# Quantisation of the feed-forward weights: started in batch 0, paced by five steps in later odd batches, its loads on SyncE's queue

## The chip, the cores and the metric

The kernel runs on one core of a Trainium2 chip. The metric is the device time of one execution in microseconds, as the median of several runs. A core has five engines that run their own instruction streams in order and wait for each other by semaphores: TensorE (PE in the profile; its weight loads are PEld), VectorE (DVE), ScalarE (ACT), GpSimd (POOL) and SyncE (SP), which here only issues transfers. GpSimd issues transfers too; those travel on another DMA queue (q0) than SyncE's (q1).

## The reference, cut to what matters

One block of a Perceiver: cross attention of 64 latents to 512 context rows in each of 16 batches, then self attention over the latents, then a feed-forward layer with FP4 weights and activations. The feed-forward layer quantises its three weight matrices in blocks of 16:

```python
def fp4_quant_dequant(x):
    xb = x.reshape(shape[:-1] + (shape[-1] // BLOCK, BLOCK))
    scale = jnp.max(jnp.abs(xb), axis=-1, keepdims=True) / 6.0
    scale = jnp.maximum(scale, jnp.float32(1e-12))
    idx = jnp.searchsorted(_MID, jnp.abs(xb / scale))
    return (_GRID[idx] * jnp.sign(xb) * scale).reshape(shape)

gate, y = fp4_linear(x, w_gate), fp4_linear(x, w_up)      # 512 -> 1408
return fp4_linear(jax.nn.silu(gate) * y, w_down)          # 1408 -> 512
```

The weights do not depend on the activations, so this quantisation can be done at any time before the feed-forward layer. Every large matrix product is computed in three fp32r terms of high and low halves (high x high, high x low, low x high).

## The kernel before, in words

The kernel has four stages in time: the latents (to 82 us), cross attention batch by batch (82 to 550), self attention and feed-forward. All instructions stand in the order in which the Python code emits them (`in_order`, L87), engine by engine; no planner moves them. An engine that waits holds up all that stands behind it on that engine.

Cross attention (`cross_attention`, L869) goes over `b` in 0 to 15. In each batch TensorE does four products for the keys (`keys(b, m)`, tile `pk`), two passes of scores (`scores(b, a)`, tile `sim`, L979), the weighted sum of the batch before (`finish(b - 1)`, tile `av`) and four products for the values (tile `pv`). Odd batches from 3 on also handle the output of an earlier pair of batches: `out_turn` (a transpose on TensorE, tile `ot`), `out_low`, `out_product` (tile `po`), `out_norm` and `out_add`, the last with three operations on GpSimd (L1163 to L1165); `out_moments` in the next even batch reads their result. The results of `keys`, `out_turn`, `out_product` and `values` share three PSUM buffers (`ps_mm`, L83), the scores share two. VectorE empties the keys (L953) and does the first half of the softmax (L1000), ScalarE empties the values (L966) and does the exponentials.

SyncE loads the context for two batches ahead: `nat` (1 MB, L322) for the statistics and four pieces `raw` (256 KB each, `fetch`, L362) of the transposed context, which ScalarE and VectorE or GpSimd split into high and low halves (L370, L376). It also turns the softmax with transposing transfers (`send`, L1050: two per pass, `far`), stores and reloads the row factors (`flat`, L350; `every`, L355), and loads the mask, the queries and the latents of the next batch (`begin`, L906, L908; `latents_values`, L920). `spread` (L339 to L341) computes the row factors on GpSimd at the end of each batch.

The quantisation (`Quantise`, L247) is cut into 35 pieces: for three column chunks of 512, 512 and 384, four pieces each of the gate and of the up matrix, then eleven of the down matrix. A piece is a generator. `tick()` advances every active piece by one step and, if it is time, starts a new one. A batch has ten places for ticks, called steps 1 to 10 here: after `keys(b, 0)`, after `keys(b, 1)`, after the flat rows, after the second scores, after `values(b, 0)`, two after the loads of the next batch, one after `out_product`, one after the fourth fetch, and one at the end of the batch. A piece's work is, by steps: the load of 128 x 512 fp32 weights into one of three buffers (L287, on GpSimd); nothing; a reduce group on VectorE (L199, L201, L202, L203); a multiplication on GpSimd (L205); a mask on VectorE and an activation on ScalarE (L208, L211); nothing; a pair on VectorE (L213, L214); a multiplication on GpSimd (L216); a transpose on VectorE and a copy on ScalarE (L296, L297); a subtraction on VectorE and the store of 512 KB (L299, L301, on GpSimd). The reduce group's operations are small but L199 must wait for the load.

A new piece starts at every fourth tick. The first tick is the last one of batch 0; batch 1 has eight. The last load is issued in step 8 of batch 14, and the last store in step 7 of batch 15.

Of the kernel before, what the change touches and what calls it, by code (L numbers as in the profile page):

```python
# [46 lines left out]
def f32(t):  # L47

    return t.bitcast(F32)
# [197 lines left out]
class Quantise:  # L247
# [3 lines left out]

    EVERY = 4

    def __init__(self, cm, sc, i):
        self.cm, self.sc = cm, sc
        self.jobs = []
        for c, (at, n) in enumerate(CHUNKS):
            for w, name in (("g", "w_gate"), ("u", "w_up")):  # L260
                self.jobs += [(w, c, k, i[name][k * P : (k + 1) * P, at : at + n]) for k in range(KC)]
        for c, (at, n) in enumerate(CHUNKS):
            self.jobs += [
                ("d", c, k, i["w_down"][at + k * P : at + (k + 1) * P, :]) for k in range(n // P)
            ]
        self.jobs.reverse()
        self.clock, self.active = 0, []

    def home(self, w1, w2):
        self.w1, self.w2 = w1, w2  # L270

    def tick(self, new=True):

        if new and self.jobs and self.clock % self.EVERY == 0:
            self.active.append(self.piece(*self.jobs.pop()))
        self.clock += 1
        self.active = [job for job in self.active if next(job, None)]

    def finish(self, all=False):
# [3 lines left out]
    def piece(self, which, c, k, src):  # L283
        cm, nc = self.cm, self.cm.nc
        name, n = f"{which}_{c}_{k}", src.shape[1]
        w = self.w2.tile([P, D], F32, tag="tri", bufs=3, name=f"qw_{name}")[:, :n]
        nc.gpsimd.dma_start(w, src)  # L287
        yield True
        yield True
        for step in cm.fp4_steps(self.w1, w, n, name, True, True):  # L290
            yield True
            if step == "relu":
                yield True
        hl = self.w1.tile([P, 2, D], F32R, tag="q_hl", name=f"qhl_{name}")[:, :, :n]
        hi, lo = hl[:, 0, :], hl[:, 1, :]
        nc.vector.transpose(f32(lo), w)  # L296
        nc.scalar.copy(hi, f32(lo))  # L297
        yield True
        nc.vector.tensor_tensor(lo, f32(lo), f32(hi), ALU.subtract)  # L299
        dst = self.sc.dn[c] if which == "d" else self.sc.gu[which, c]  # L300
        nc.gpsimd.dma_start(dst[:, :, k, :], f32(hl))  # L301
# [567 lines left out]
def cross_attention(tc, cm, sc, i, cw, cx, w1, w2, att, quant):  # L869

    nc = tc.nc
# [19 lines left out]
    def columns_of(r):  # L891

        first = S * (1 - r)
        return slice(first, first + N + S), slice(S - first, S - first + N)
# [27 lines left out]
    def mask(b):  # L922
        if b < B:
            nc.scalar.activation(
                masks[b % 2][:, S : S + N], state[b]["mu"], AF.Identity, bias=cm.masked, scale=MASKED
            )
# [17 lines left out]
    def keys(b, m):  # L944

        k = ends[b, m // 2][:, m % 2, :]
        hi, lo = cx.done[b]
        cols = slice(m * P, (m + 1) * P)
        ps = cm.mm(f"pk_{b}_{m}")
        cm.product(  # L950
            ps, lambda c: (w_k[0][:, c, cols], w_k[1][:, c, cols], hi[:, c, :], lo[:, c, :]), range(KC)
        )
        nc.vector.tensor_tensor(k[:, S : S + N], ps, cx.row[b], ALU.mult)  # L953
        state[b]["k"].append(k)
# [14 lines left out]
    def scores(b, a):  # L969

        st = state[b]
        st["sim", a] = pss = [cm.two(f"sim_{b}_{a}_{r}") for r in range(2)]
        for h in range(2):
            for r in range(2):
                rows = slice(r * S, (r + 1) * S)
                at = columns_of(r)[0].start + h * half
                for c in range(2):
                    m = 2 * a + c
                    nc.tensor.matmul(  # L979
                        pss[r][c * S : (c + 1) * S, h, :half],  # L980
                        lhsT=queries[b % 2][rows, m, :],
                        rhs=st["k"][m][rows, at : at + half],
                        start=True,
                        stop=True,
                    )

    def softmax(b, a):
        st = state[b]
        both = w1.tile([P, 2 * (N + S)], F32, tag="pr", bufs=2, name=f"pr_{b}_{a}")
        st["whole", a] = both  # L990
        st["pr", a] = both.rearrange("p (r n) -> p r n", r=2)

        def two(t):
            return t.rearrange("p (h n) -> p h n", h=2)

        for r, ps in enumerate(st.pop(("sim", a))):
            mask = masks[b % 2][:, columns_of(r)[0]]
            pr = st["pr", a][:, r, :]
            least = cm.small.tile([P, 1], F32, tag="least", name=f"least_{b}_{a}_{r}")
            nc.vector.tensor_tensor_reduce(  # L1000
                two(pr), ps[:, :, :half], two(mask), -1.0, BIG, ALU.add, ALU.min, least
            )
            t = 2 * a + r
            nc.scalar.activation(  # L1004
                pr, pr, AF.Exp, bias=least, scale=-1.0, accum_out=st["tot"][:, t : t + 1]
            )
# [160 lines left out]
    def out_moments(p):  # L1167
        cm.shift(cm.x[p], f"a_{p}", cm.x_mv[:, p, :])
# [8 lines left out]
    def weight_o(k):  # L1177
        raw = raw_o.pop(k)
        cm.split(w_o[0][:, k, :], w_o[1][:, k, :], raw, nc.gpsimd)
# [18 lines left out]
    cx.load(2)  # L1198
    for b in range(B):

        def tick():
            if b:
                quant.tick()

        done = (b - 3) // 2 if b >= 3 and b % 2 else None
        last = b == B - 1
        keys(b, 0)
        if b:
            cx.load(b + 2)
        if last:  # L1210
            att.load("Wq")
            att.load("Wk")
        cx.high(b + 1, 0)
        if b >= 4 and b % 2 == 0:
            out_moments((b - 4) // 2)
        if b > 1:
            tick()
        if done is not None:
            out_turn(done)
        keys(b, 1)  # L1220
        cx.low(b + 1, 0)
        cx.high(b + 1, 1)
        if b:
            join(b - 1, 0)
        if b > 1:
            tick()
        keys(b, 2)
        if b:
            mask(b)
        if done is not None:  # L1230
            out_low(done)
        cx.fetch(b + 2, 0)
        if b == 0:
            for k in range(KC):
                load_o(k)
        cx.flat(b + 1)
        cx.low(b + 1, 1)
        cx.high(b + 1, 2)
        if b:
            join(b - 1, 1)  # L1240
        tick()
        if last:
            att.split("Wq", 0, 1)
        if b == 0:
            scores(b, 0)
            softmax(b, 0)
        keys(b, 3)
        cx.fetch(b + 2, 1)
        if b:
            scores(b, 0)  # L1250
            softmax(b, 0)
        cx.low(b + 1, 2)
        cx.high(b + 1, 3)
        if b:
            finish(b - 1)
            scores(b, 1)
            softmax(b, 1)
            around(b + 1, 1)
            around(b + 2, 0)
        tick()  # L1260
        values(b, 0)
        if b and not last:
            halves(b, 0)
        cx.every(b + 1)
        cx.low(b + 1, 3)
        cx.stats(b + 2, 0)
        tick()
        if last:
            att.split("Wq", 2, 3)
            att.load("Wv")  # L1270
        if b == 0:
            scores(b, 1)
            softmax(b, 1)
            around(b + 1, 1)
            around(b + 2, 0)
        values(b, 1)
        if b == 0:
            halves(b, 0)
        if not last:
            turn_latents(b)  # L1280
            halves(b, 1)
            send(b, 0)
        begin(b + 1)
        latents_values(b + 1)
        cx.fetch(b + 2, 2)
        cx.stats(b + 2, 1)
        tick()
        if last:
            att.norm(0)
            att.split("Wk", 0, 1)  # L1290
        tick()
        if done is not None:
            out_product(done)
        tick()
        values(b, 2)
        if not last:
            send(b, 1)
        cx.fetch(b + 2, 3)
        cx.stats(b + 2, 2)
        tick()  # L1300
        if done is not None:
            out_norm(done)
            out_add(done)
        if b == 0:
            weight_o(0)
            weight_o(1)
        if b == 5:
            att.sa.work()
        if last:
            att.split("Wk", 2, 3)  # L1310
            att.load("Wo")
            att.turn(0)
        values(b, 3)
        cx.stats(b + 2, 3)
        cx.spread(b + 2)
        if b == 0:
            weight_o(2)
            weight_o(3)
        quant.tick()
# [693 lines left out]
```

## Time and profile before

| | us |
|---|---|
| median of 3 runs | 878.34 (876.41 to 878.44) |
| the profiled execution | 878.15 |
| its span, first to last instruction | 876.4 |
| TensorE busy | 859.5 (98%) |
| VectorE busy | 690.3 (79%) |
| ScalarE busy | 486.4 (56%) |
| GpSimd busy | 345.6 (39%) |
| mean granted TensorE clock | 0.996 |

The profile is of one execution on the chip. Some 2 us lie outside its span. A timeline row gives the start, the length, the engine, the source line, the operation, the tiles written and read, shapes, the number of instructions merged and, in brackets, how long the engine sat idle before and what ended that. A row of a table of stretches gives start:end and length, then the busy time and number of instructions of PE, PEld, DVE, ACT and POOL, the granted clock, the DMA engines' share and GB/s. TensorE's ends are modelled, so back-to-back rows overlap slightly. For SyncE a row is the issue of a transfer; its landing is not in the profile.

### The profile page before, as it was taken

How to read it: one execution, taken by the hardware profiler on the slowest of the kernel's cores; microseconds unless marked ns; L12 is line 12 of the kernel's file. 1: busy time of each engine (PE TensorE's matmuls, PEld its weight loads, DVE VectorE, ACT ScalarE, POOL GpSimd, SP SyncE). 2: the span in 40 equal slices, each digit the busy share in tenths (PEclk: the TensorE clock that was granted, in tenths of full speed). 3: DMA queues.
4: the chain of work that ended last, by engine and by line, in shares of the span. 5: the costliest groups of instructions: out<-in, count | busy, mean ns of one | idle time of the engine just before them, and what ended most of it. 6: DMA issues, size and time to landing. Idle time of an engine off the chain costs nothing.

```text
span 876.4 us, 16721 instructions
## 1 busy us (share of the span) xinstructions
PE 859.5 (98%) x6263; PEld 706.9 (81%) x6263; DVE 690.3 (79%) x1457; ACT 486.4 (56%) x847; POOL 345.6 (39%) x413
## 2 busy tenths in 40 slices
PE   9999999999999999999999999999999999999998
PEld 8988777887887777778877877878888888888886
DVE  7734457988789877887897776698998898888876
ACT  5654675766758757667767576544556232332221
POOL 3334144546465474364654733555543120111100
PEclk9999999999999999999999999999999999999999
DMA  7664767775975777668857564150008330000000
GB/s 243 207 229 170 198 183 202 207 190 182 235 186 154 216 211 202 168 177 224 192 148 211 159 162 182 49 193 2 2 1 336 121 144 24 1 13 13 13 13 24
DMA packets 135607, 126.79 MB, mean 145 GB/s; under 512 B 95512, under 2 KB 98472, under 8 KB 134248
## 3 DMA queue, kind: packets, MB, share of 16 engines
q1 hardware_dynamic: 127912, 99.26, 39.2%
q0 software_dynamic: 7616, 26.48, 9.3%
q8 instruction: 49, 0.80, 0.4%
q14 instruction: 30, 0.25, 0.1%
HBM read 84.26 MB, written 25.72 MB: 125 GB/s over the span
## 4 chain that ended last, share of the span: by engine, by line
PE 84%; DVE 7%; POOL 3%; ACT 2%; DMA 2%; issue 1%; DVEq 0%; POOLq 0%; ACTq 0%
PE pv L126 18%; PE pk L126 14%; PE gu L126 14%; PE dn L126 7%; PE sim L979 4%; PE av L1101 3%; PE Wv L126 3%; PE wo L126 3%; PE lv L126 2%; PE Wq L126 2%; PE Wk L126 2%; PE lq L126 2%; PE lk L126 2%; PE po L126 1%; PE ht L176 1%
## 5 line engine op out<-in xcount | busy, mean ns | idle before, releaser
L126 PE MATMUL pv<-xvh,x 128*128 128x512 f32 x512 | 136.9, 399 | 0.3 <-ACT v L966 0.3
L126 PE MATMUL pk<-x,xkh 128*128 128x512 f32 x512 | 127.2, 390 | 0.0
L126 PEld LDWEIGHTS pv<-xvh,x 128*128 128x128 f32 x512 | 95.2, 190 | 26.8 <-issue 7.3
L126 PEld LDWEIGHTS pk<-x,xkh 128*128 128x128 f32 x512 | 95.5, 188 | 19.8 <-issue 0.4
L1004 ACT ACTIVATE pr<-pr,least 128x576 f32<-128x576 f32 x64 | 49.1, 769 | 60.0 <-DVE least L1000 60.0
L953 DVE TENSOR_TENSOR k<-pk,row 128x512 f32<-128x512 f32 x64 | 42.9, 671 | 39.1 <-PE pk L126 31.6
L126 PE MATMUL pv<-xvl,x 128*128 128x512 f32 x256 | 70.0, 396 | 0.0
L126 PE MATMUL pk<-x,xkl 128*128 128x512 f32 x256 | 68.5, 389 | 0.0
L1060 ACT COPY prT<-far 128x1024 uint16<-128x1024 uint16 x60 | 67.3, 1173 | 1.3 <-DMA far<-half 1.3
L126 PE MATMUL gu<-uT,fx 128*128 128x512 f32 (+1 forms) x288 | 66.8, 377 | 0.0
L966 ACT ACTIVATE v<-pv,rs 128x512 f32<-128x512 f32 x64 | 43.9, 685 | 41.1 <-PE pv L126 40.1
L126 PE MATMUL gu<-gT,fx 128*128 128x512 f32 (+1 forms) x288 | 65.8, 376 | 0.0
L376 POOL TENSOR_TENSOR x<-raw,x 128x512 fp32r<-128x512 f32 x32 | 41.8, 1306 | 55.3 <-ACT x L370 47.4
L1040 ACT COPY half<-pr 128x1024 uint16<-128x1024 uint16 x60 | 59.8, 1048 | 0.0
L126 PEld LDWEIGHTS gu<-gT,fx 128*128 128x128 f32 x288 | 52.2, 188 | 7.6 <-ACT fx L134 0.2
L126 PEld LDWEIGHTS pv<-xvl,x 128*128 128x128 f32 x256 | 49.1, 192 | 11.0
L126 PEld LDWEIGHTS gu<-uT,fx 128*128 128x128 f32 x288 | 51.9, 188 | 7.2
L126 PEld LDWEIGHTS pk<-x,xkl 128*128 128x128 f32 x256 | 48.1, 188 | 10.0
L979 PE MATMUL sim<-k,mask 64*64 64x288 f32 x512 | 43.8, 418 | 9.3 <-DVE least L1000 7.9
L1000 DVE CUSTOM_DVE_ANT_0 pr<-sim,mask 128x576 f32<-128x576 f32 x64 | 45.8, 753 | 5.7 <-PE sim L979 2.8
L211 ACT ACTIVATE qe_h<-qe_h,mmagic 128x512 f32<-128x512 f32 (+1 forms) x24 | 16.5, 688 | 59.1 <-DVE qe_h L208 56.9
L126 PE MATMUL dn<-dT,hh 128*128 128x512 f32 x170 | 42.9, 392 | 0.0
(357 smaller groups left out, 1942.1 us busy)
## 6 DMA issues: line engine op xcount, KB each, us to landing
nat<-in_ctx_dram SPq DMA_DIRECT2D x16, 1024.0 KB
raw<-in_ctxT_dram SPq DMA_DIRECT2D x64, 256.0 KB
d_d<-qhl_d POOLq DMA_DIRECT2D x11, 512.0 KB, 3.8
row<-rs_d SPq DMA_DIRECT2D x16, 256.0 KB
g_d<-qhl_g POOLq DMA_DIRECT2D x8, 512.0 KB, 4.4
u_d<-qhl_u POOLq DMA_DIRECT2D x8, 512.0 KB, 4.6
gT<-g_d SPq DMA_DIRECT2D x4, 1024.0 KB
uT<-u_d SPq DMA_DIRECT2D x4, 1024.0 KB
```

The source lines that it names most:

```text
L126: self.nc.tensor.matmul(ps, lhsT=p[i], rhs=p[j], start=start and n == 0, stop=stop and n == last)
L176: self.nc.tensor.transpose(pt[:, c * P : (c + 1) * P], src[:, c * P : (c + 1) * P], self.ident)
L211: nc.scalar.activation(e, e, AF.Relu, bias=self.mmagic, scale=MAGIC)
L376: by.tensor_tensor(lo, self.raw[:, c, :], f32(hi), ALU.subtract)
L953: nc.vector.tensor_tensor(k[:, S : S + N], ps, cx.row[b], ALU.mult)
L966: nc.scalar.mul(v, ps, cx.rs[b][:, t : t + 1])
L979: nc.tensor.matmul(pss[r][c * S : (c + 1) * S, h, :half], lhsT=queries[b % 2][rows, m, :], rhs=st["k"][m][rows, at : at + half], start=Tru ...
L1000: nc.vector.tensor_tensor_reduce(two(pr), ps[:, :, :half], two(mask), -1.0, BIG, ALU.add, ALU.min, least)
L1004: nc.scalar.activation(pr, pr, AF.Exp, bias=least, scale=-1.0, accum_out=st["tot"][:, t : t + 1])
L1040: nc.scalar.copy(half, src[:, h])
L1060: nc.scalar.copy(dst, src)
L1101: nc.tensor.matmul(st["av"][r][rows, a, :], lhsT=prT[:, j, rows], rhs=st["v"][j][:, at : at + S], start=False, stop=j == NJ - 1, skip_grou ...
```

## The change

Four things change. (1) Ticks count from batch 0 on, eight of them there, and batch 1 has all ten; the first load is issued in step 3 of batch 0. (2) A new piece starts when `every` ticks have passed since the last start: 4, but 5 in batches 7, 9, 11 and 13. (3) A piece's load is issued by SyncE instead of GpSimd, and one more empty step stands between it and the reduce group. (4) In batch 0 the first scores and their softmax stand behind `keys(0, 3)`, as they do in all other batches.

By step, loads are issued in batch 0 in steps 3 and 7; in 1, 3, 5, 8 and 12 in steps 1, 5 and 9; in 2, 4, 6, 10 and 14 in steps 3 and 7; in 7 and 11 in steps 2 and 7; in 9 and 13 in steps 4 and 9. The reduce group follows three steps later, so that of a load in step 7 stands in step 10. In batches 2 to 6 all other work of the pieces stands in the same steps as before. The last load is in step 7 of batch 14, the last store in step 7 of batch 15 as before.

In SyncE's order the load of step 1 stands behind `nat`, that of step 3 behind `flat`, of step 5 behind `every`, of step 7 behind `send(b, 0)`, `begin`, `latents_values` and the third fetch and ahead of `send(b, 1)`, and of step 9 behind the fourth fetch and ahead of the next `nat`.

```diff
 class Quantise:
-    EVERY = 4
-
     def __init__(self, cm, sc, i):
 ...
-        self.clock, self.active = 0, []
+        self.every, self.since, self.active = 4, 3, []
 ...
     def tick(self, new=True):
 
-        if new and self.jobs and self.clock % self.EVERY == 0:
+        self.since += 1
+        if new and self.jobs and self.since >= self.every:
             self.active.append(self.piece(*self.jobs.pop()))
-        self.clock += 1
+            self.since = 0
         self.active = [job for job in self.active if next(job, None)]
 ...
     def piece(self, which, c, k, src):
         cm, nc = self.cm, self.cm.nc
         name, n = f"{which}_{c}_{k}", src.shape[1]
         w = self.w2.tile([P, D], F32, tag="tri", bufs=3, name=f"qw_{name}")[:, :n]
-        nc.gpsimd.dma_start(w, src)
+        nc.sync.dma_start(w, src)
+        yield True
         yield True
         yield True
         for step in cm.fp4_steps(self.w1, w, n, name, True, True):
 ...
     for b in range(B):
 
-        def tick():
-            if b:
-                quant.tick()
-
+        tick = quant.tick
+        quant.every = 4 + (b % 2 if 6 < b < 14 else 0)
 ...
-        if b > 1:
+        if b:
             tick()
         if done is not None:
             out_turn(done)
 ...
-        if b > 1:
+        if b:
             tick()
         keys(b, 2)
 ...
-        if b == 0:
-            scores(b, 0)
-            softmax(b, 0)
         keys(b, 3)
         cx.fetch(b + 2, 1)
-        if b:
-            scores(b, 0)
-            softmax(b, 0)
+        scores(b, 0)
+        softmax(b, 0)
         cx.low(b + 1, 2)
```

## The prediction

> **What bounds the kernel now.** I read the page first. TensorE is busy nearly all the time, so a change can only win what TensorE loses now, or lose more.
>
> ```profile
> span 876.4 us, 16721 instructions
> PE 859.5 (98%) x6263; PEld 706.9 (81%) x6263; DVE 690.3 (79%) x1457; ACT 486.4 (56%) x847; POOL 345.6 (39%) x413
> ```
>
> The waits of PE come next. Each row gives total, times and longest. Only the score matmuls (sim) wait for anything that counts: six times for VectorE's softmax, once for a transfer.
>
> ```profile
> PE sim L979 <- DVE least L1000: 7.9, 6, 1.6
> PE sim L979 <- DMA mask<-q_d: 1.4, 1, 1.4
> ```
>
> Then the stretches, one per batch, cut at each batch's first pk matmul (start:end, length, PE busy and so on; the clock follows POOL). These are batches 1, 2, 4, 5 and 10.
>
> ```profile
> 108.18:134.97 26.79, 26.79 (x211) 21.51 (x210) 13.94 (x32) 19.41 (x31) 11.63 (x13) 1.00 0.69 177
> 134.97:164.02 29.05, 27.48 (x212) 21.68 (x210) 24.11 (x55) 20.16 (x32) 13.58 (x16) 1.00 0.69 186
> 193.99:224.50 30.51, 29.05 (x212) 22.59 (x210) 26.67 (x58) 20.41 (x32) 19.13 (x23) 0.94 0.65 181
> 224.50:254.46 29.96, 29.96 (x228) 24.16 (x226) 23.57 (x53) 20.49 (x34) 13.48 (x16) 1.00 0.79 210
> 371.33:398.78 27.45, 27.45 (x211) 21.68 (x210) 23.57 (x56) 19.56 (x32) 16.47 (x22) 1.00 0.67 179
> ```
>
> An even batch has the matmuls of batch 1, which runs without a gap in 26.79 us. Above that, batches 2 to 14 by twos take 2.26, 3.72, 1.77, 1.60, 0.66, 3.78 and 2.16, together 15.95 us. Odd batches 3 to 13 all take 29.96 or 29.97 without a gap. So the loss sits in even batches, and the timelines say why. PE:
>
> ```profile
> 150.96 1.87 PE L979 MATMUL sim<-k,mask 64*64 64x288 f32 x16 [1.56 <-DVE least L1000]
> 209.87 2.19 PE L979 MATMUL sim<-k,mask 64*64 64x288 f32 x16 [1.46 <-DVE least L1000]
> 230.39 1.98 PE L126 MATMUL pk<-x,xkh 128*128 128x512 f32 x8
> ```
>
> An undisturbed sim pass takes 1.20, so each stall costs its gap plus some 0.7 to 1.0. VectorE in batches 2, 4 and 5:
>
> ```profile
> 147.47 0.69 DVE L199 TENSOR_REDUCE qm_g<-qw_g 128x32 f32<-128x512 f32 x1 [2.95 <-DMA qw_g<-in_w_gate_dram]
> 204.49 0.69 DVE L199 TENSOR_REDUCE qm_u<-qw_u 128x32 f32<-128x512 f32 x1 [0.58 <-DMA qw_u<-in_w_up_dram]
> 205.21 2.08 DVE L201 SCALAR_TENSOR_TENSOR qs_u<-qm_u,least 128x32 f32<-128x32 f32 x1
> 225.62 0.69 DVE L199 TENSOR_REDUCE qm_g<-qw_g 128x32 f32<-128x512 f32 x1 [0.41 <-DMA qw_g<-in_w_gate_dram]
> ```
>
> GpSimd, and SyncE's queue:
>
> ```profile
> 201.45 0.65 POOL L287 DMA_DIRECT2D qw_u<-in_w_up_dram  x1
> 204.88 1.35 POOL L376 TENSOR_TENSOR x<-raw,x 128x512 fp32r<-128x512 f32 x1
> 206.12 1.12 POOL L216 TENSOR_TENSOR qw_u<-qw_u,qs_u 128x512 f32<-128x512 f32 x1
> ```
>
> ```profile
> 224.48 0.76 SPq L362 DMA_DIRECT2D raw<-in_ctxT_dram  x1
> 225.34 3.67 SPq L1050 DMA_TRANSPOSE far<-half  x2
> ```
>
> GpSimd issues a load only when its own work lets it (201.45, behind out_add and spread), and the load lands late. But in batch 4 VectorE waits just 0.58 for it. The larger loss is L201: 32 columns wide, it takes 0.19 when alone and 2.08 here, ending at 207.29 as GpSimd's L216 ends at 207.24. The late load is all of the trouble only in batch 2 (2.95).
>
> **The change, part by part** (gains and losses against the profiled execution, 878.15 us, which is 0.19 under the median of 878.34).
>
> *Scores of batch 0 behind keys(0, 3).* The third keys product, 2.72 us, now covers the 1.38 wait for the mask and queries, and the sim pass falls from 1.59 to 1.20: -1.77. If the transfer were 1.3 later, the cover would be gone.
>
> *Earlier loads for the second step of even batches.* In batches 2, 4 and 6 the steps fall on the same places as before; the only difference is that this piece's load is issued in the odd batch's ninth step, behind the fourth fetch (196.39 in batch 4, against 201.45). It lands some 4 us earlier. Batch 2 has no other cause: -2.26. In batches 4 and 6 GpSimd is freed of one 0.65 issue, so L376, L216 and with them L201 end 0.65 earlier: -0.65 each. Batch 4 also stops losing clock (below): -1.26 more. Bounds for both together: 0 to their 5.49.
>
> *A piece per five steps in odd batches 7, 9, 11, 13.* Before, a pair of L213/L214 (1.3) and a reduce group (0.60 + 0.88 + 0.19 + 0.35) stood ahead of out_norm; in 7 and 11 only the pair does, so out_add starts 2.0 earlier. In batches 8 and 12 the steps between the keys hold a transpose, a subtract and a mask (0.65, 0.66, 0.38) where a pair and a slow reduce group (some 4.5) stood: VectorE is 2.8 ahead, more than the stalls: -1.60 and -3.5 of 3.78. In 10 and 14 the pair runs one step sooner, so L216 precedes L376 and frees L201 some 1.3 earlier: -0.66 and -1.6 of 2.16. Bounds: a gain of all 8.20; a loss of 1.4, if the loads of 7 and 11 take 7.5 us (priced below) and hold up the fourth keys product of 8 and 12 by 0.7 each.
>
> Gains: 1.77 + 2.26 + 1.91 + 0.65 + 1.60 + 0.66 + 3.5 + 1.6 = 13.95.
>
> *Loads in SyncE's queue.* 35 issues of about 0.6 leave GpSimd (22 us at 39% busy, hidden apart from the 0.65 counted) and enter SyncE, which is in order. Loads of all steps but the seventh have 7 us or more until their reduce (196.95 to 203.9 for step 9 in batch 3, 209.9 to 218.1 for step 3 in batch 4) and cost nothing; behind them fetches and row loads move by 0.6 and are needed a batch later. The buffer each waits for was freed three steps before. The load of step 7 is different: in batches 0, 2, 4, 6, 10 and 14 (and 7, 11) its reduce is step 10, the last VectorE work before the next batch's first key eviction, and SyncE reaches it only behind two transposes, four loads and the third fetch, at 225.3 in the example, 0.8 us after batch 5 began and about when VectorE now wants the data. Where the stall is gone the slot is as after batch 1, where the same fetch ends at 135.50, +0.6; in batch 7 it was +1.3, and I take +1.0. From landing to the end of the key eviction took 2.07 in batch 2 (147.47 to 149.54). The third keys product of an odd batch (230.39, +5.89) needs the buffer of the first, because the turn of o holds the third. So landing later than +3.82 stalls TensorE one for one.
>
> No row shows this load's landing on this queue. Bounds are 2.7 and 7.5, the fastest and slowest load through GpSimd's. I take 4.0: their medians, 3.1 to 3.3, plus 0.8 for the equal fetch just ahead (256 KB at 336 GB/s, the page's highest slice). Landing is then +4.6 to +5.0, the stall 0.8, 1.0, 1.2, 0.8, 0.8 in batches 3, 5, 7, 11, 15: 4.5. In batch 1 the slot is 111.3 (+3.1), the buffer is needed by the fourth product (116.34), so landing at 115.3 costs 1.0. In 8 and 12 the slot is 0.7 before the batch begins; no cost. VectorE is idle 4 to 8 us in every odd batch (its busy column against the length) and catches up before softmax. The transposes behind move 0.6; ScalarE joins them 5 us later. Losses: 5.5 (bounds 0 and 26).
>
> *Clock.* In batches 4 and 12 the clock is 0.94 over the batch, 0.50 in the stretch 212 to 214, after a gap of 1.46; the batches 2 and 14 with like gaps kept 1.00. Two of the seven gaps above 0.9 cost 1.3 each, so I charge the six new ones one: 1.3. The Trainium skill (TensorE: Matmul & The Clock Gate, What's actually happening) has the clock fall after an idle window of about 3.4 us; by that rule neither the old nor the new stalls would cost clock, and the forecast would be the same to 0.1 us, since 1.26 and 1.3 nearly cancel.
>
> The same skill (DMA: Bandwidth & Descriptors, Issuing engines are not separate DMA queues) speaks against this change: all issuers share 16 DMA engines, and moving an issue saves only sequencer time. Taken alone, the rule makes the new queue worth nothing in itself and the gains those of earlier issue, 864.4; the price of standing in line is mine, from rows.
>
> Sum: -13.95 + 5.5 + 1.3 = -7.15, or 871.0; against the median, **871.2 us**.
>
> **Rivals.**
> 1. *The step-7 loads are hidden.* Landing in 2.7 is +3.3 to +3.7, under +3.82: no losses but a few tenths. For it: in batch 1, with no stores about, the fourth fetch and transposes pass at once. Against: GpSimd's 512 KB stores share the DMA engines at batch ends (one is issued at 223.40 in batch 4). 878.3 - 13.95 + 0.5 = 865.
> 2. *The even stalls stay.* L201 is blocked by GpSimd whenever it comes, and VectorE waits 1.97 for out_add in batch 4 whatever the load does. Then only batches 0, 2 and a clock loss go: -5.3, against 5.5 lost: 878, no change.
> 3. *Slower: the step-7 loads take 7.5*, as GpSimd's slowest did (139.93 to 147.45). Landing +8.1 stalls batches 3, 5, 7, 11 and 15 by some 4.3 each and batch 1 by 4.5: 26 lost, 13.95 won, 892 with one clock loss. It decides from a landing time of 5.5 us on, where six losses of 2.1 and the clock eat the gains. For it: they stand behind 256-byte-row transfers; against: the median.
>
> **How the numbers follow.** The forecast has 0.42 (its own range 868 to 876), rival 1 0.25, rival 2 0.18, rival 3 0.15. The range 864 to 881 leaves out most of rival 3 and the low end of rival 1. A measurement here tells 0.3% (2.6 us) from no change: faster means under 875.7. That takes rival 1 and most of the forecast, 0.66; same 0.18; slower 0.16.
>
> **What will show it.** Right: no [.. <-DMA mask<-q_d] before a sim; even batches 2, 8, 12 near 26.8; L199 of the last step waiting 2 to 4 us for its load at the ends of batches 2, 4, 6, 10, 14, and PE idle before the third pk of batches 3, 5, 7, 11, 15 on a key eviction; L201 near 1.4 in 4 and 6. Wrong: odd batches still at 29.96 (rival 1), even ones still long (rival 2), or odd ones over 32 (rival 3). Work after 550 us should not change.

## The result, and the profile after

The changed kernel takes 880.44 us (median of 13 runs, 877.70 to 883.24); the kernel before takes 877.14 beside it. The ratio is 1.0039 with a 95% interval of 1.0023 to 1.0055: 0.4% slower, where 871.2 and faster was forecast. The profiled execution took 880.43, with a span of 878.7; all that follows compares it with the profiled execution before (878.15, span 876.4).

The page of the changed kernel, and who TensorE waited for (total, times, longest):

```profile
span 878.7 us, 16718 instructions
PE 857.1 (98%) x6263; PEld 705.3 (80%) x6263; DVE 685.9 (78%) x1457; ACT 487.6 (55%) x847; POOL 327.1 (37%) x378
```

```profile
PE pk L126 <- DVE k L953: 12.0, 6, 2.8
PE sim L979 <- DVE least L1000: 1.6, 2, 1.1
```

The waits of the score matmuls, 7.9 + 1.4 before, are down to 1.6. A new wait has taken their place: six times a keys product waits 12.0 us in all for VectorE to empty a buffer. GpSimd lost its 35 issues (345.6 to 327.1 busy); what that relief is worth is seen in x5_hybrid below.

The stretches of the changed kernel, for the same batches 1, 2, 4, 5 and 10 as before the change:

```profile
106.40:136.29 29.89, 27.49 (x211) 21.60 (x210) 20.68 (x45) 21.68 (x35) 15.30 (x15) 1.00 0.71 191
136.29:163.08 26.79, 26.79 (x212) 21.51 (x210) 25.33 (x56) 20.32 (x32) 11.98 (x14) 1.00 0.77 222
...
195.46:223.49 28.03, 27.48 (x211) 21.68 (x210) 24.82 (x55) 20.19 (x32) 16.22 (x18) 1.00 0.68 190
223.49:258.13 34.64, 31.85 (x227) 25.22 (x226) 24.56 (x57) 20.75 (x35) 13.81 (x15) 0.95 0.72 191
...
375.75:402.54 26.79, 26.79 (x212) 21.51 (x210) 21.24 (x49) 19.06 (x30) 14.19 (x18) 1.00 0.67 172
```

Batches 2 and 10 now run at the 26.79 of an undisturbed even batch; batch 4, at 28.03, is still 1.2 above it. Batches 1 and 5, clean before (26.79 and 29.96), are 3.1 and 4.7 longer. Over all batches, after less before:

| batch | 0 | 1 | 2 | 3 | 4 | 5 | 6 | 7 | 8 | 9 | 10 | 11 | 12 | 13 | 14 | 15 |
|---|---|---|---|---|---|---|---|---|---|---|---|---|---|---|---|---|
| us | -1.85 | +3.10 | -2.26 | +2.41 | -2.48 | +4.68 | -0.01 | +2.36 | -1.60 | 0 | -0.66 | +2.31 | -2.85 | +0.32 | -2.16 | +1.59 |

The even batches won 13.9, the odd ones lost 16.8; some 0.6 was won behind cross attention, so that the span grew by 2.3. Of the 16.8, 12.0 is the wait above; the other 4.8 is in TensorE's slower passes after the waits (PE busy 30.30 in place of 29.96 in batch 3, 31.85 in batch 5 with the clock at 0.95) and in batches 1 and 13.

One such place, the end of batch 4, in SyncE's queue, on VectorE and on TensorE:

```profile
221.61 0.57 SPq L906 DMA_DIRECT2D mu<-in_mask_dram  x1
222.23 0.57 SPq L908 DMA_DIRECT2D mask<-q_d  x1
222.84 1.28 SPq L920 DMA_DIRECT2D lat<-v_d  x2
224.22 0.54 SPq L362 DMA_DIRECT2D raw<-in_ctxT_dram  x1
224.87 0.37 SPq L286 DMA_DIRECT2D qw_g<-in_w_gate_dram  x1
225.34 4.73 SPq L1050 DMA_TRANSPOSE far<-half  x2
```

```profile
225.07 0.69 DVE L214 SCALAR_TENSOR_TENSOR qw_g<-qw_g,qe_g 128x512 f32<-128x512 f32 x1
230.21 0.69 DVE L199 TENSOR_REDUCE qm_g<-qw_g 128x32 f32<-128x512 f32 x1 [4.45 <-DMA qw_g<-in_w_gate_dram]
...
231.65 1.22 DVE L953 TENSOR_TENSOR k<-pk,row 128x512 f32<-128x512 f32 x2
```

```profile
232.33 3.68 PE L126 MATMUL pk<-x,xkh 128*128 128x512 f32 x8 [2.79 <-DVE k L953]
```

The load of step 7 is issued at 224.87, behind mask, queries, latents and the third fetch. VectorE is free for its reduce at 225.76 and gets the data at 230.21. The key evictions stand behind that reduce, so two finished products lie in PSUM until 231.65, and the third starts only at 232.33. The pass that follows takes 3.68 in place of 1.98: the granted clock is 0.50 from 232.4 to 235.8. The chain of work that ended last holds a load of step 7 six times; its rows give the issue and the time to landing:

```profile
164.01 5.06 DMA qw_u<-in_w_up_dram
...
224.87 5.32 DMA qw_g<-in_w_gate_dram
...
288.05 4.80 DMA qw_g<-in_w_gate_dram
...
403.76 4.65 DMA qw_d<-in_w_down_dram
...
432.73 4.70 DMA qw_d<-in_w_down_dram
...
520.37 4.40 DMA qw_d<-in_w_down_dram
```

Five of them stand at the end of an even batch. The one at 432.73 ends batch 11, and batch 12 takes 27.72 with it as it does below with the loads on GpSimd.

### The profile page after: what moved, and what is told of

Same layout as the page of the kernel before. It is cut to its first block, busy times and chain, and to the rows that moved or that the text cites. A ratio compares the mean times of both kernels' runs of the same rounds, so it can differ in the third digit from the quotient of the medians.

```text
span 878.7 us, 16718 instructions
## 1 busy us (share of the span) xinstructions
PE 857.1 (98%) x6263; PEld 705.3 (80%) x6263; DVE 685.9 (78%) x1457; ACT 487.6 (55%) x847; POOL 327.1 (37%) x378
## 4 chain that ended last, share of the span: by engine, by line
PE 75%; DVE 11%; ACT 4%; DMA 4%; POOL 3%; issue 2%; SPq 1%; DVEq 0%; POOLq 0%; ACTq 0%
PE gu L126 14%; PE pk L126 12%; PE pv L126 12%; PE dn L126 7%; PE sim L979 4%; PE av L1101 3%; PE Wv L126 3%; PE wo L126 3%; PE lv L126 2%; PE Wq L126 2%; PE Wk L126 2%; PE lq L126 2%; PE lk L126 2%; DMA qw_d<-in_w_down_dram 2%; PE po L126 2%
## 5 line engine op out<-in xcount | busy, mean ns | idle before, releaser
L126 PE MATMUL pk<-x,xkh 128*128 128x512 f32 x512 | 129.5, 395 | 12.0 <-DVE k L953 12.0
L376 POOL TENSOR_TENSOR x<-raw,x 128x512 fp32r<-128x512 f32 x32 | 44.2, 1381 | 57.7 <-ACT x L370 57.7
L329 DVE BATCH_NORM_STATS2 cst<-nat 128x6 f32<-128x512 f32 x64 | 42.8, 669 | 1.0 <-DMA nat<-in_ctx_dram 1.0
```

The source lines that it names most:

```text
L126: self.nc.tensor.matmul(ps, lhsT=p[i], rhs=p[j], start=start and n == 0, stop=stop and n == last)
L329: nc.vector.bn_stats(st, self.nat[b][:, j, :])
L376: by.tensor_tensor(lo, self.raw[:, c, :], f32(hi), ALU.subtract)
```

## The experiments

One table holds most of what follows: medians by who issues the loads, how many steps ahead of use, and with which pacing.

| pacing | GpSimd, 2 ahead | GpSimd, 3 ahead | SyncE, 2 ahead | SyncE, 3 ahead |
|---|---|---|---|---|
| as before | 877 (before) | 869.84 | 921.24 | |
| from batch 0, four steps | | 868.50 | | |
| as changed | 872.83 | **866.20** | | 880.44 (changed) |

### The loads back on GpSimd (x1_gpsimd)

In the changed kernel:

```diff
-        nc.sync.dma_start(w, src)
+        nc.gpsimd.dma_start(w, src)
```

> The changed kernel with one word different: the loads are issued by GpSimd again, still 3 steps ahead of use. Theory (landing): the changed kernel won about 13.9 us in batches 0, 2, 4, 8, 10, 12 and 14 and lost about 16.8 in batches 1, 3, 5, 7, 11 and 15, all of it because VectorE waits at the end of the batch before for the load of step 7, which SyncE issues late and which lands 3.2 to 5.3 us after that. GpSimd's own work lets it issue this load at about 221.8 in batch 4 (behind its product that ends at 221.78) instead of 224.87, so it is there by about 225.5, when VectorE wants it (225.76): batches 3, 5, 7 and 11 go back to about 30.0 us, 15 to about 32.2, and PE waits for no key eviction. The 0.65 of each issue comes back on GpSimd in batches 4, 6, 8 to 14, worth 1 to 3 us together. 880.4 - 16.8 + 2 = about 866 (863 to 870). Rival (pacing): the queue does not matter, and batches 1, 3, 5, 7, 11 are long because the reduce of step 10 now stands right ahead of the first key eviction, with VectorE late from other work: 877 to 882, the odd batches still 32 or more.

Measured: 866.20 us (865.79 to 866.85), ratio to the kernel before 0.988 (0.9856 to 0.9903): 14.2 faster than the changed kernel, in the middle of what the landing theory gave. Batches 3, 4 and 5:

```profile
161.08:191.04 29.96, 29.96 (x227) 24.17 (x226) 24.92 (x56) 20.49 (x34) 14.47 (x17) 1.00 0.81 213
191.04:219.23 28.19, 27.49 (x211) 21.69 (x210) 24.98 (x55) 20.18 (x32) 17.88 (x21) 1.00 0.70 189
219.23:249.26 30.03, 30.03 (x228) 24.23 (x226) 26.09 (x57) 20.53 (x35) 14.53 (x17) 1.00 0.81 219
```

No keys product waits any more. The same load of batch 4, on GpSimd and on VectorE:

```profile
216.45 1.06 POOL L205 TENSOR_TENSOR qw_g<-qw_g,qm_g 128x512 f32<-128x512 f32 x1 [0.74 <-DVE qm_g L203]
217.45 0.64 POOL L286 DMA_DIRECT2D qw_g<-in_w_gate_dram  x1
```

```profile
222.03 0.69 DVE L199 TENSOR_REDUCE qm_g<-qw_g 128x32 f32<-128x512 f32 x1 [0.55 <-DMA qw_g<-in_w_gate_dram]
```

It is there 4.6 us after its issue, 0.7 sooner than on SyncE's queue. What GpSimd offers is above all an earlier place: 1.78 before the batch ends, where SyncE came to it 1.38 after. The rival (pacing) falls.

### The load ahead of the sends, still on SyncE (x2_early)

```diff
+    def start(self):
+        if not self.early:
+            job = self.piece(*self.jobs.pop())
+            next(job)
+            self.early.append(job)
+
+    def ahead(self, n):
+        if self.jobs and self.since + n >= self.every:
+            self.start()
...
         nc.sync.dma_start(w, src)
+        yield True
...
             halves(b, 1)
+            quant.ahead(2)
             send(b, 0)
```

`ahead(2)` issues the load now if its step is one of the next two; `tick` (its lines are left out here) takes the piece over when that step comes, and one more empty step keeps its reduce where it was. An earlier form of this edit, x2_ahead, left the last piece unfinished and gave no time.

> The changed kernel with the loads still on SyncE's queue, but the load of step 6 or 7 issued ahead of the first send of that batch, that is ahead of its two transposes, the four loads for the next batch and the third fetch. Every reduce stays on its step. Theory (place in the queue): SyncE has nothing to issue between 214.67 and 218.92 in batch 4, so this load goes some 10 us earlier than 224.87; VectorE waits nowhere for it, and the odd batches go back to about 30.0 as they did with the loads on GpSimd (x1_gpsimd: 866.2), with nothing added on GpSimd: 864.6 (862 to 867). Rival (transfers): what delays the load is not its place in line but that this queue also carries the fetches, row loads and transposes, whose packets fill it: then it lands late wherever it stands, and of the 14.2 us between the changed kernel and x1_gpsimd at most half comes back: 873 to 880.

Measured: 866.91 us (866.23 to 869.83), ratio 0.9891 (0.9871 to 0.9912). SyncE's queue at the end of batch 4 (other line numbers, since the kernel is longer):

```profile
211.95 0.34 SPq L298 DMA_DIRECT2D qw_g<-in_w_gate_dram  x1
215.91 2.64 SPq L1063 DMA_TRANSPOSE far<-half  x2
```

The load passes while SyncE has nothing to do, and batches 3, 5, 7 and 11 take 29.96. So the rival (transfers) falls: it is the place in the queue that cost 13.5 us. Batch 1 (29.07) stays long: GpSimd is busy with low halves of the output weights until about 114.9, the first piece is late on VectorE and ScalarE, and the joins on ScalarE behind it hold up the weighted sum by 1.5. Which of these is the cause these rows don't show; z_split below takes two of the low halves off GpSimd.

### Only the loads of steps 6 and 7 on GpSimd (x5_hybrid)

```diff
-        nc.sync.dma_start(w, src)
+        self.queue.dma_start(w, src)
...
         cx.stats(b + 2, 1)
+        quant.queue = nc.gpsimd
         tick()
...
         tick()
+        quant.queue = nc.sync
```

> The changed kernel with only the loads of steps 6 and 7 issued by GpSimd, all others by SyncE. Theory: as in x1_gpsimd the odd batches are free of stalls; as in the changed kernel GpSimd is spared the issue ahead of its product in batches 4 and 6 (28.03 and 28.55 there, 28.19 and 28.76 in x1_gpsimd), so 865.7 (863.5 to 867.5), 0.5 under x1_gpsimd and hardly to be told from it. Rival: the other loads too cost something on SyncE's queue (rows, fetches and transposes behind them go later): 868 to 872.

Measured: 867.02 us (866.09 to 868.67), ratio 0.9884 (0.9864 to 0.9904). Batches 4 and 6 fell to 28.03 and 28.57 as expected, but batch 1 took 30.67, part of it at half clock. It can't be told from the first experiment. Behind batch 1 the other loads show no cost where the change put them. In batch 1, here and in x2_early, VectorE's mask (L208) takes 1.5 in place of 0.43, beside GpSimd's L376, which now starts at once (116.90 here) and not behind the issue of a load (117.30 in x1_gpsimd). The weighted sum then waits 1.5 in place of 0.43. So the relief of GpSimd seems to cost 1.1 in batch 1, which takes 29.07 and 30.67 in these two and 27.98 to 28.15 in the kernels with all early loads on GpSimd; in batches 4 and 6 it brought 0.2 each.

### The third fetch behind the load (x3_swap)

```diff
-        cx.fetch(b + 2, 2)
         cx.stats(b + 2, 1)
         tick()
...
         tick()
+        cx.fetch(b + 2, 2)
```

> The changed kernel with the third fetch put behind the load of step 7 instead of ahead of it, nothing else. It tells what makes that load land late. Theory (landing behind the fetch): in batch 4 the fetch's 128 packets of 2 KB go from 225.8 to about 228.0 and the load's 128 from there to about 229.7, in the order of issue; the load put first is issued 0.65 earlier and its packets start some 2.2 earlier, so it lands 2 to 2.8 us earlier. The stalls of batches 3, 7 and 11 (about 2.0 each) vanish, that of batch 5 (2.79) falls under 0.8, and of the 16.8 lost 10 to 15 come back: 867 to 870. Rival (landing behind the transposes): the load ends when the two transposes issued right behind it end (169.09 against 168.93 in batch 2, 230.21 against 230.07 in batch 4), and the swap gains only the 0.65 of the issue slot in six batches: 876 to 878.

Measured: 873.75 us (872.50 to 875.81), ratio 0.9968 (0.9953 to 0.9983), between the two expectations. The waits for key evictions fell from 12.0 to 5.3:

```profile
PE pk L126 <- DVE k L953: 5.3, 5, 1.5
```

The load at the end of batch 2 was used 3.27 after its issue in place of 5.08, and TensorE waited 0.36 in batch 3 in place of 2.08. At the end of batch 4 the chain gives only 0.7 less than before the swap, and the issue itself stands 0.6 earlier (0.75 after the batch's end in place of 1.38):

```profile
222.37 4.64 DMA qw_g<-in_w_gate_dram
```

The fetch ahead explains about half of the loss: 6.7 us came back of the 14.2 that the first experiment found. The transposes issued behind the load do not hold it: at the end of batch 2 it was used at 167.11, while SyncE was still at them until 169.17.

### The pieces' stores one step later (z_store)

In the changed kernel:

```diff
         nc.vector.tensor_tensor(lo, f32(lo), f32(hi), ALU.subtract)
+        yield True
         dst = self.sc.dn[c] if which == "d" else self.sc.gu[which, c]
         nc.gpsimd.dma_start(dst[:, :, k, :], f32(hl))
```

> The changed kernel, SyncE's queue and order untouched, with the store of each finished piece (512 KB, GpSimd's queue) one step later. In x3_swap the load of batch 4, put ahead of the fetch, was issued at 222.37 and still landed only at 227.0, while the store of the piece before, issued at 222.09, moved its 4 KB packets from 223.25 to 226. It tells whether that store, which falls on the last microseconds of an even batch, is what stretches the landing. Theory (store): without it fetch and load take about 0.9 each once the small rows are through, so in batch 4 the load lands at about 227.6 in place of 230.2, and 1.5 to 2.5 come back in each of batches 3, 5, 7, 11 and 15: 871 (867 to 875). Rival (place in the queue alone): transposes, rows and fetch ahead cost the same with or without the store: 878 to 882.

Measured: 878.07 us (875.03 to 880.76), ratio 1.001 (0.9993 to 1.0026). At the end of batch 4 the load was issued at 225.50 and used at 228.84:

```profile
228.84 0.69 DVE L199 TENSOR_REDUCE qm_g<-qw_g 128x32 f32<-128x512 f32 x1 [2.46 <-DMA qw_g<-in_w_gate_dram]
```

That is 3.34 in place of 5.34; batches 2, 6 and 11 have 3.45, 3.44 and 3.49 in place of 5.08, 4.83 and 4.72. So there the 512 KB store on the other queue does stretch the landing. At the ends of batches 7, 10 and 14 it still took 5.5, 4.8 and 3.9 (5.2, 4.7 and 4.4 before the edit). In the changed kernel a store is issued 0.9 to 2.2 ahead of the load in all seven places. The edit puts it behind the load in batches 2, 4, 6, 10 and 11, but not in 7 and 14, where the loads are issued at 314.14 and 521.16 and the stores still stand ahead of them (the line is 302 here):

```profile
313.92 0.72 POOL L302 DMA_DIRECT2D g_d<-qhl_g  x1
...
518.94 0.69 POOL L302 DMA_DIRECT2D d_d<-qhl_d  x1 [2.39 <-DVE qhl_d L299]
```

So the theory holds for four of the five loads that the edit freed of the store; the one of batch 10 (store 0.9 behind the load, still 4.8) stays open. It is no remedy all the same: the waits for key evictions fell from 12.0 to 6.1, but those of the score passes rose from 1.6 to 2.8 and those of the weighted sums from 1.1 to 3.1, and the clock fell twice (0.94 in batch 6, 0.95 in batch 11) in place of once. Batches 4, 6, 8 and 12 got 0.8 to 2.4 longer than in the changed kernel. Why those waits grew was not followed.

### The queue alone (y1_queue)

In the kernel before, 2 steps ahead as it was:

```diff
-        nc.gpsimd.dma_start(w, src)
+        nc.sync.dma_start(w, src)
```

> The kernel before with the loads on SyncE's queue and nothing else: still 2 steps ahead, the old pacing. It prices the queue alone. Theory (place in line): the load of step 8 in even batches stands behind the second send and the fourth fetch, so it is issued at about 170.8 in batch 2 and lands at about 174 to 175, where VectorE wants it at 165.8 and the third keys product can do with a landing up to 3.82 after the start of the next batch (167.8): 6 to 7 us lost in each of batches 3, 5, 7, 9, 11, 13, 15; the load of step 6 in odd batches is issued about 1 us after the second batch end and holds up the keys of even batches by 0 to 3. 878 + 45 to 60 = about 930 (905 to 960). Rival (the queue is only an address): moving the issue saves GpSimd its 0.65 and changes nothing else: 874 to 879.

Measured: 921.24 us (917.58 to 926.22), ratio 1.0506 (1.0472 to 1.054), as expected in sum, not in its parts. Batches 3, 4 and 5:

```profile
162.87:195.59 32.72, 30.25 (x227) 24.10 (x226) 22.71 (x53) 20.74 (x35) 13.83 (x15) 1.00 0.70 190
195.59:230.93 35.34, 31.49 (x211) 24.21 (x210) 27.72 (x61) 20.41 (x32) 17.23 (x20) 0.90 0.56 158
230.93:262.69 31.76, 30.31 (x228) 24.10 (x226) 21.19 (x49) 20.58 (x34) 12.79 (x14) 1.00 0.74 198
```

The odd batches from 3 to 13 lose 1 to 4, not 6 to 7: step 8 stands ahead of the second send, not behind it, which the expectation had wrong. From batch 4 on the even ones lose 3 to 7, since the load of step 6 in an odd batch reaches VectorE about 3 us into the next batch (198.60 in batch 4), and the reduce holds up keys and softmax together. The rival (only an address) falls by 44 us.

### One step earlier, the rest as before (y2_early)

In the kernel before:

```diff
-        if new and self.jobs and self.clock % self.EVERY == 0:
+        if new and self.jobs and (self.clock == 0 or self.clock % self.EVERY == 3):
...
         nc.gpsimd.dma_start(w, src)
+        yield True
```

> The kernel before with the loads on GpSimd's queue, but 3 steps ahead (the first one still in batch 0's last step, all others one step earlier than before, so that every reduce but the first stays on its step). It prices the earlier load alone, without the new pacing and without SyncE's queue. Theory: the load is there when VectorE comes to it, batch 2 falls from 29.05 to about 26.8, batch 4 by 0.6 to 1.9, batch 6 by 0 to 0.6, and the stalls of batches 8 to 14 stay, which are due to the crowding on VectorE and GpSimd: 878 - 3.5 = about 874 (871 to 877). Rival (the late load is behind all even stalls): batches 8, 12 and 14 fall too, 866 to 870.

Measured: 869.84 us (868.37 to 870.69), ratio 0.9915 (0.9893 to 0.9936): the rival's range. Batches 2, 4, 8, 10, 12 and 14:

```profile
135.46:162.77 27.31, 27.31 (x211) 21.69 (x210) 22.36 (x49) 20.16 (x32) 11.91 (x14) 1.00 0.69 195
192.78:220.97 28.19, 27.50 (x211) 21.69 (x210) 24.99 (x55) 20.19 (x32) 17.87 (x21) 1.00 0.74 190
309.72:337.23 27.51, 27.49 (x211) 21.70 (x210) 24.35 (x58) 19.68 (x32) 17.28 (x23) 1.00 0.65 182
367.19:394.32 27.13, 27.13 (x212) 21.77 (x210) 24.05 (x56) 19.56 (x32) 17.10 (x23) 1.00 0.66 178
424.28:452.79 28.51, 27.50 (x211) 21.69 (x210) 25.30 (x55) 20.17 (x32) 17.98 (x21) 1.00 0.75 184
482.75:510.94 28.19, 27.49 (x212) 21.69 (x210) 23.83 (x50) 20.21 (x32) 18.19 (x22) 1.00 0.48 127
```

All of them fall, 12 by 2.06 and 8 by 0.88, with the old pacing. The earlier load brought about 8 us in these batches, some 2.5 of it the clock that batches 4 and 12 had lost before (0.94 there). The execution as a whole shows 7.5 less than the one before: batch 0 took 1.8 less, with no wait for its transfer, but cross attention began 2.3 later (83.90, where before has 81.62).

### The pacing alone (x4_pace), and the five steps alone (z_four)

```diff
-        self.every, self.since, self.active = 4, 3, []
+        self.every, self.since, self.active = 4, 2, []
...
-        nc.sync.dma_start(w, src)
-        yield True
+        nc.gpsimd.dma_start(w, src)
```

> The kernel before with the pacing alone (from batch 0 on, 5 steps in odd batches 7 to 13, scores of batch 0 behind the fourth keys product), every reduce on the step it has in the changed kernel, but loads on GpSimd's queue 2 steps ahead as before. It tells which of the gains come from the earlier load. Theory: batches 0, 8, 10, 12 and 14 gain as in the changed kernel (1.85, 1.6, 0.7, 2.9, 2.2), while batch 2 keeps its 2.26 and batch 4 its 3.72 of stalls, since there the load again waits for GpSimd's work; batches 3, 5, 7, 11 stay at 29.96. 878.15 - 9.2 = 869 (866 to 873). Rival (pacing): the losses of the odd batches come from the pacing, 880 to 890.

Measured: 872.83 us (869.55 to 875.12), ratio 0.9949 (0.9929 to 0.9968), at the edge of the range. The gains in 0, 8, 12 and 14 came; not foreseen were 31.56 and 32.06 in batches 9 and 13. In batch 9 VectorE waits for two loads:

```profile
348.77 0.55 DVE L199 TENSOR_REDUCE qm_u<-qw_u 128x24 f32<-128x384 f32 x1 [2.20 <-DMA qw_u<-in_w_up_dram]
363.79 0.55 DVE L199 TENSOR_REDUCE qm_u<-qw_u 128x24 f32<-128x384 f32 x1 [2.96 <-DMA qw_u<-in_w_up_dram]
```

And the five steps taken out of the first experiment's kernel:

```diff
-        quant.every = 4 + (b % 2 if 6 < b < 14 else 0)
+        quant.every = 4
```

> x1_gpsimd (loads on GpSimd, 3 steps ahead) without the five-step pacing: a piece every 4 steps in all batches. It prices the pacing by itself. By the prediction's sum the pacing brings 1.60 + 0.66 + 3.5 + 1.6 = 7.36 in batches 8 to 14, which makes 866.2 + 7.4 = 873.6. By y2_early, where the earlier load alone took batches 8, 10, 12 and 14 to 27.51, 27.13, 28.51 and 28.19 (x1_gpsimd: 26.79, 26.79, 27.72, 26.79) and left batch 13 at 29.96 (30.23), it brings 3.2 - 0.3 = 2.9: 869.1 (868 to 870.5).

Measured: 868.50 us (868.06 to 869.94), ratio 0.9907 (0.9888 to 0.9926). Against 866.20 the five-step pacing brings 2.3. Its batches 8, 10, 12 and 14 take 27.16, 27.27, 28.53 and 28.20, 3.1 more than with five steps; 0.8 of that is given back in batches 13 and 15.

### The scores of batch 0 in their old place (z_scores)

In the kernel of the first experiment:

```diff
+        if b == 0:
+            scores(b, 0)
+            softmax(b, 0)
         keys(b, 3)
         cx.fetch(b + 2, 1)
-        scores(b, 0)
-        softmax(b, 0)
+        if b:
+            scores(b, 0)
+            softmax(b, 0)
```

> x1_gpsimd with the scores of batch 0 ahead of its fourth keys product, as in the kernel before. By the prediction the move is worth 1.77 (a wait of 1.38 for the transfer of mask and queries and a slower score pass): 866.2 + 1.8 = 868.0, batch 0 at 26.5. Rival (the wait was an accident of that one execution): y1_queue and y2_early kept the old order, and there batch 0 takes 24.72 and 24.78 with no wait for the transfer: 866.2, batch 0 at 24.7.

Measured: 867.70 us (866.53 to 868.88), ratio 0.9897 (0.9877 to 0.9916), against 866.20. Batch 0 took 25.27, and the wait is there, but short:

```profile
90.54 1.49 PE L979 MATMUL sim<-k,mask 64*64 64x288 f32 x16 [0.17 <-DMA mask<-q_d]
```

The old order costs 1.85 in the execution before, 0.55 here, and nothing in the two executions named in the expectation. The move is a safeguard worth 0 to 1.85, and these runs don't say what it is worth on average.

### Two low halves of the output weights on VectorE (z_split)

In the kernel of the first experiment:

```diff
-        cm.split(w_o[0][:, k, :], w_o[1][:, k, :], raw, nc.gpsimd)
+        cm.split(w_o[0][:, k, :], w_o[1][:, k, :], raw, (nc.vector, nc.gpsimd)[k > 1])
```

> x1_gpsimd with two of the four low halves of the output weights (in batch 0) on VectorE in place of GpSimd. In x1_gpsimd batch 1 takes 28.00 in place of 26.79, since GpSimd comes to the first piece's second product only at 114.62, behind four of these low halves (107.34 to 114.66), and VectorE's transpose, ScalarE's copy and the join behind it wait for that. Theory: two less free GpSimd 2.7 earlier, batch 1 falls to 26.8 to 27.2, 865.2 (864 to 866.5), the best of all kernels here. Rival: VectorE then waits for ScalarE's casts (to about 108.0) ahead of the first key eviction of batch 1 and gives the gain back there: 866 to 867.5.

Measured: 866.04 us (865.86 to 867.79), ratio 0.9881 (0.986 to 0.9902). Batch 1 takes 28.15, no shorter; the gain did not come. GpSimd was free early, but its next work, the row factors, now waits for VectorE's statistics, which stand behind the two low halves there:

```profile
109.88 0.53 POOL L339 TENSOR_SCALAR rs<-cmv 128x4 f32<-128x4 f32 x1 [6.09 <-DVE cmv L330]
```

It came to the piece's second product at 114.71, no sooner than the 114.62 of x1_gpsimd. That is the rival, by another path than it named; what else keeps batch 1 long stays open.

## Why the prediction was wrong

**The landing of the step-7 loads was mis-sized.** This is the step that failed: landing at +4.6 to +5.0 after the start of the odd batch, a slot of +0.6 to +1.0 plus 4.0. The mechanism was right: slot plus landing less 3.82 is what TensorE waits. In batches 3, 5, 7, 11 and 15 that is 0.93 + 5.06 - 3.82 = 2.17, then 2.88, 2.35, 2.05 and 1.36; TensorE waited 2.08, 2.79, 2.07, 1.97 and 1.28. But both terms were too small. The landing took 4.4 to 5.3, not 4.0, 4.2 more over the five. The slots were +0.78 to +1.38, 2.1 more over the five. So the data came at +5.2 to +6.7, and the five stalls cost 10.2 in place of 4.5. The 4.0 was the median of all loads on GpSimd's queue (3.1 to 3.3) plus 0.8. The trace before had better rows. The loads that GpSimd issues in the last microseconds of an even batch, and the reduces that wait for them:

```profile
162.25 0.64 POOL L287 DMA_DIRECT2D qw_u<-in_w_up_dram  x1
...
281.21 0.64 POOL L287 DMA_DIRECT2D qw_u<-in_w_up_dram  x1
...
455.92 0.64 POOL L287 DMA_DIRECT2D qw_d<-in_w_down_dram  x1
```

```profile
166.93 0.69 DVE L199 TENSOR_REDUCE qm_u<-qw_u 128x32 f32<-128x512 f32 x1 [0.64 <-DMA qw_u<-in_w_up_dram]
...
286.29 0.69 DVE L199 TENSOR_REDUCE qm_u<-qw_u 128x32 f32<-128x512 f32 x1 [1.05 <-DMA qw_u<-in_w_up_dram]
...
461.07 0.69 DVE L199 TENSOR_REDUCE qm_d<-qw_d 128x32 f32<-128x512 f32 x1 [1.03 <-DMA qw_d<-in_w_down_dram]
```

They are there 4.68, 5.08 and 5.15 after the issue. These are the slowest of seven; behind batches 4, 8, 10 and 14 it is 4.45, 4.38, 4.21 and 3.36. A load at that place in a batch lands late on either queue; the median over all places hid it. The median of the seven, 4.45, would have made the five stalls 6.8 with the slots as taken, still short of 10.2.

**Batch 1: a small operation was taken at its undisturbed length.** Counted from the start of the batch, the load came as forecast (+7.2; forecast +7.1), though from a later slot (+4.0, not +3.1) and with a shorter landing (3.2, not 4.0): luck. But L201, behind it on VectorE, took 1.02 beside GpSimd's L216, where 0.19 was counted:

```profile
114.34 1.02 DVE L201 SCALAR_TENSOR_TENSOR qs_g<-qm_g,least 128x32 f32<-128x32 f32 x1
```

1.0 was forecast, 1.85 waited.

**What a stall costs beyond its gap was left out.** The passes after each gap took 0.3 more, 0.7 in batch 1 with two gaps, 1.9 in batch 5 with its clock loss; the joins of batch 1 took 0.55. The prediction had measured the like for the score passes (0.7 to 1.0) and not charged it for the keys. The one clock loss charged at 1.3 came, at about 1.6.

The loads of the other steps had as little as 3.5 us until their reduce (496.15 to 499.65), where 7 or more was counted, but VectorE waited for none of them behind batch 0.

Together: of the 9.4 us between 871.0 and the profiled 880.43, the five stalls are 5.7, batch 1 is 2.1, the slower passes of the other odd batches 1.9 beyond the 1.3 charged, and batch 13 0.3; the gains fell short by 0.1, and some 0.6 was won behind cross attention.

**The gains were right in sum and wrong in cause.** 13.95 was forecast; the even batches show 13.9, one by one within 0.65. But the five-step pacing was given 7.36 of it, and on top of the earlier load it is worth 2.3 (z_four). The earlier load was given 4.8, all in batches 2, 4 and 6; without the new pacing (y2_early) it brought 3.8 there and 4.0 in batches 8 to 14. Both remove the same stalls, so what each brings depends on whether the other is there. In batches 4 and 6, L201 was to fall to 1.4 and bring 0.65 each; it took 1.83 and 1.76, and batch 6 kept its stall (1.06 before the scores) and gained nothing, while batch 4 gained more than forecast. And the 1.77 for the scores of batch 0 removed a wait that the old order does not always have.

**The rivals.** Rival 3 (slower) had the mechanism, with a landing of 7.5 and a turning point of 5.5; it turned at 4.4 to 5.3 because the slots were later and the stalls cost more than their gaps. Rival 1, 865 with the loads hidden, is the time of the kernels that hide them: 866.2 and 866.9. Rival 2 (the even stalls stay) is refuted by batches 2, 8 and 10, though it holds for batch 6.

The Trainium skill (DMA: Bandwidth & Descriptors, Issuing engines are not separate DMA queues) states that all issuers share the same DMA engines and that another issuer saves only its sequencer's time. The runs agree with the first half: at the end of batch 4 a store on GpSimd's queue stretched a load on SyncE's from 3.3 to 5.3. The second half misses what decided here, 13.5 us by the load's place in its issuer's own program order (x2_early). The same page (Issuing engine by pattern) gives plain loads to SyncE and calls that path generally faster; at the end of batch 4 the load took 5.3 there and 4.6 from GpSimd, at an earlier time.

## What to carry to other kernels

Before a transfer is moved to another in-order issuer, write down what that issuer does at the moment of issue, and take the landing time from transfers at the same place in the loop, not from a median over all places. A wait put ahead of an eviction is paid on the PSUM buffers: slot plus landing less the slack, taken from the trace afterwards, gives each stall within 0.1 to 0.3 us. The place in the issuer's own order matters more than the queue: the same three-step lead took 866.2 from GpSimd, 866.9 from an early place on SyncE, and 880.4 from a late one.

## What the runs showed of the hardware

The granted clock halved after a gap of 2.79 in batch 5 and not after gaps of 2.08, 2.07 and 1.97 of the same kind; before the change it had done so after 1.46, and in z_store it did after 1.90 in batch 11, a gap of the same kind. The kernel with the queue alone, whose batches 4 and 8 stood still for 3.9 and 2.9 in all, has 0.90 in both. A gap's length does not decide it alone. The Trainium skill (TensorE: Matmul & The Clock Gate, What's actually happening) has the clock fall after an idle window of about 3.4 us; of the gaps here with a fall, those of 1.46, 1.90 and 2.79 are shorter.
